# Context attention of a perceiver block: compacting a tile's outputs and repeating their sums by transfers through device memory

## The chip, the cores and the metric

The kernel runs on one core of one Trainium2 chip, as one program. The metric is the device time of one execution in microseconds (us); the median of several runs counts. A profile of one further execution comes with it; its times are from the start of its span.

## The reference, cut to what matters

Two layers of a perceiver work on 32 batches of 64 latent rows with 256 channels, with a context of 1601 rows of 256 channels for each batch. The second layer begins with the attention that this change is about:

```
q = layernorm(x) @ WqT + bq          # 64 rows per batch, 16 heads of 16
k = ctx @ WkT + bk                   # 1601 rows
v = ctx @ WvT                        # 1601 rows; bv is applied with the output projection
p = exp(q k / 4 - max)               # per head
o = (p v) / sum(p)                   # 64 rows x 16 heads x 16
x = x + (o + bv) @ WoT + bo
```

Before it stand a context mean, a self attention with 16 heads and a small routed feed-forward; behind it a recurrent mixer, a gated feed-forward and a quantised feed-forward. All of them run on the same engines, interleaved with the attention.

## The kernel before

**Tiles and steps.** Two batches make a tile of 128 rows, so there are 16 tiles. A tile's context is worked off in 13 steps (`NU = 13`): 12 steps of 512 context rows for one batch and one half of the heads, and one step (number 9) for the 65 rows that are left of both batches. The loop runs over 208 steps `g`; in the text a step is told by its number 0 to 12 within its tile.

**Inside a step**, in this order on every engine:

- `column_scores(g)`: the maxima as a first matmul (L773, tile `s`), then the scores with context rows on the partitions (L779), then two `Exp` by ScalarE into `pt` (L785).
- `values(g+4)`: eight fp32 matmuls into `vps` (L233), copied by VectorE into `vau` (L715). A head has 16 columns in `vau`, followed by a column of ones, so that the next product yields the head's sum as a 17th row.
- a piece of normalising in some steps (below), then pieces of the other layers that a plan puts here (`run(g, 0)`).
- `row_scores(g+5)`: scores with queries on the partitions (L731, tile `r`), reduced by VectorE to maxima `mx` (L738).
- `weighted(g)`: 32 small matmuls of `pt` with `vau` into `w.o` (L803), accumulated in PSUM over all steps of the tile.
- `keys(g+6)`: matmuls into `kps` (L233), copied with their bias into `kt` by ScalarE (L698).
- in step 1 the projection of the tile before, and further pieces of the plan (`run(g, 1)`).

**Order.** PE, VectorE, ScalarE and GpSimd keep the order in which the program writes their instructions; the order of the transfers on SP's queue is left to the scheduler. Each engine works in its order.

**PSUM.** `s` and `r` share two buffers of two banks (`ps_sc`), `w.o` has one bank (`ps_o`). Everything else (`vps`, `kps`, `sums`, `wo`, `hg`, `tpp` and so on) takes the next of three buffers in rotation (`ps_mm`), and a matmul into it waits until what lay in it three tiles ago has been read.

**Outputs of a tile.** `w.o` has four groups q, one for each batch and half of the heads; a group holds two sets m of four heads beside each other. Each head has 32 partitions, of which 16 are outputs, the 17th is the sum and 15 are not used. VectorE copies groups 0 to 2 to `osb` after step 9 (L808) and group 3 after step 12 (L810). `normalise(pos, q)` runs in steps 10, 11 and 12 for groups 0 to 2 and in step 0 of the next tile for group 3: a matmul with a 0/1 matrix `sel` repeats each sum over the 32 partitions of its head (L818, tile `sums`), VectorE takes reciprocals of 128x128 (L821) and multiplies (L822) into `oT`. `projected` then multiplies `oT` with `w_o2` in four matmuls (L838), because half of the 512 rows of `oT` and `w_o2` are padding, and adds the residue (L841). `out_bias` does the same once with the bias of the values (L830). At the end of the program, after step 12 of the last tile, group 3 is normalised and projected right away, and the last two tiles' second layers run off with nothing beside them.

**Loads.** SP issues the context (`ctxT`, 1.6 MB each), a second copy of it by halves (`part`, 800 KB) that ScalarE sums for the first layer's mean (L245), the 65 rows (`rest`), `x`, weights, and the output rows.

Of the kernel before, what the change touches and what calls it, by code (L numbers as in the profile page):

```python
# [9 lines left out]
F32 = mybir.dt.float32  # L10
BF16 = mybir.dt.bfloat16
AF = mybir.ActivationFunctionType
ALU = mybir.AluOpType
AX = mybir.AxisListType

P = 128
NB = 32
S = 64
D = 256
L = 1601  # L20
H = 16
NT = NB * S // P
# [6 lines left out]
NP = L // PIECE  # L29
TAIL = L - NP * PIECE  # L30
NU = 4 * NP + 1
# [7 lines left out]
BQ, BK, BV, BQ2, BK2, BV2, GC, GG, GF, DWB, DW = range(11)  # L39
# [5 lines left out]
def perceiver_kernel(ctx: ExitStack, tc: tile.TileContext, a: dict, out: bass.AP):  # L45
    nc = tc.nc
    PSUM = bass.MemoryType.PSUM

    const = ctx.enter_context(tc.tile_pool(name="const", bufs=1))
# [5 lines left out]
    loop = ctx.enter_context(ExitStack())  # L55
    big = loop.enter_context(tc.tile_pool(name="big", bufs=1))
    ps_sc = loop.enter_context(tc.tile_pool(name="ps_sc", bufs=2, space=PSUM))
    ps_o = loop.enter_context(tc.tile_pool(name="ps_o", bufs=1, space=PSUM))


# [8 lines left out]
    def mm_tile(shape, name, dtype=F32):  # L69
        return ps_mm.tile(shape, dtype, tag="mm", name=name)  # L70
# [32 lines left out]
    def load_rest(ti):  # L103

        t = big.tile([P, 2, 2, TAIL], F32, tag="rest", name=f"rest_{ti}", bufs=2)
        for b in range(2):
# [32 lines left out]

    onesb = const.tile([P, P], BF16, name="onesb")  # L140
    nc.vector.memset(onesb, 1.0)
    sel = const.tile([P, 4, 32], F32, name="sel")
    nc.gpsimd.affine_select(out=sel, in_=ones.rearrange("p (j r) -> p j r", j=4), compare_op=ALU.is_equal, fill=0.0,
                            base=-16, pattern=[[-32, 4], [0, 32]], channel_multiplier=1)


    dist = work_tile([P, S], "xn", "dist")
    for hb in range(2):
# [639 lines left out]
    def weighted(g):  # L788

        pos, h, k = split(g)  # L790
        w = wholes[pos]
        first, last = g % NU == 0, g % NU == NU - 1
        if first:
            w.o = o_tile([P, 4, 2, S], f"o1_{w.ti}")
        v, pts = vau[g % 5], w.pt.pop(g)
        kr = TAIL if h is None else P
        for j in range(4):
            q = j if h is None else h % 4
            for m in range(2):
                for c in range(4):  # L800
                    hd = 4 * m + c

                    nc.tensor.matmul(w.o[32 * c:32 * c + 32, q, m, :], lhsT=v[:kr, j, 17 * hd:17 * hd + 32],  # L803
                                     rhs=pts[m][:kr, c // 2, j, c % 2 * S:c % 2 * S + S],
                                     start=(m == 0 and (first and j == 0 or h is None and j == 3)), stop=(m == 1 and (last and j == 3 or h is None and j == 2)))
        if h is None:
            w.osb = work.tile([P, 4, 2, S], F32, tag="osb", name=f"osb_{w.ti}", bufs=1)
            nc.vector.tensor_copy(w.osb[:, 0:3], w.o[:, 0:3])  # L808
        elif last:
            nc.vector.tensor_copy(w.osb[:, 3], w.o[:, 3])  # L810

    def normalise(pos, q):

        w = wholes[pos]
        if q == 0:
            w.oT = work.tile([P, 2, 2, 2, S], F32, tag="oT1", name=f"oT1_{w.ti}", bufs=1)
        t = mm_tile([P, 2, S], f"sums_{w.ti}_{q}")
        nc.tensor.matmul(t.rearrange("p m s -> p (m s)"), lhsT=sel.rearrange("p j r -> p (j r)"),  # L818
                         rhs=w.osb[:, q].rearrange("p m s -> p (m s)"), start=True, stop=True)
        rs = work.tile([P, 2, S], F32, tag="rm", name=f"rs_{w.ti}_{q}", bufs=1)  # L820
        nc.vector.reciprocal(rs, t)  # L821
        nc.vector.tensor_tensor(w.oT[:, q % 2, :, q // 2, :], w.osb[:, q], rs, ALU.mult)  # L822

    def out_bias():

        bvb = work.tile([P, 4, P], F32, tag="oT1", name="bvb", bufs=1)
        nc.vector.tensor_copy(bvb, bv2.unsqueeze(2).to_broadcast([P, 4, P]))
        o = mm_tile([P, D], "bo2")
        for g in range(4):
            nc.tensor.matmul(o, lhsT=bvb[:, g, :], rhs=w_o2[:, g, :], start=(g == 0), stop=(g == 3))  # L830
        nc.vector.tensor_tensor(rows[:, R_BO2:R_BO2 + D], o, rows[:, R_BO2:R_BO2 + D], ALU.add)

    def projected(pos):

        w = wholes[pos]
        o = mm_tile([P, D], f"wo1_{w.ti}")
        for g in range(4):
            nc.tensor.matmul(o, lhsT=w.oT[:, g // 2, g % 2].rearrange("p b s -> p (b s)"), rhs=w_o2[:, g, :],  # L838
                             start=(g == 0), stop=(g == 3))
        x = work.tile([P, D], F32, tag="x4", name=f"x4_{w.ti}", bufs=1)  # L840
        nc.vector.tensor_tensor(x, o, residues[pos], ALU.add)  # L841
        return x
# [187 lines left out]
    w_s2 = load_w("L0_ffn_sw2T", D)  # L1030
    w_q2 = load_w("L1_xattn_WqT", D)


    w_o2 = const.tile([P, 4, D], F32, name="w_o2")
    bv2 = const.tile([P, 4], F32, name="bv2")
    nc.gpsimd.memset(w_o2, 0.0)
    nc.gpsimd.memset(bv2, 0.0)
    w_pw = const.tile([P, 2, D], F32, name="w_pw")
    w_hg = const.tile([P, 2, 2 * DI], F32, name="w_hg")
    w_go = const.tile([P, 4, 64], F32, name="w_go")  # L1040
# [6 lines left out]
    nc.gpsimd.memset(w_fo[:, NF - 1, :], 0.0)  # L1047

    def late_weights():
        for j in range(4):  # L1050
            nc.sync.dma_start(w_o2[32 * j:32 * j + 16],
                              a["L1_xattn_WoT"].rearrange("(g j d) o -> j d g o", j=4, d=16)[j])
            nc.sync.dma_start(bv2[32 * j:32 * j + 16], a["bv2"][j])
        nc.sync.dma_start(w_pw, a["L1_attn_pw_wT"].rearrange("(c p) o -> p c o", p=P))
        nc.sync.dma_start(w_hg, a["L1_attn_w_hg"].rearrange("(c h) d e -> (h d) c e", c=2))
        nc.sync.dma_start(w_go[:DI], a["L1_attn_w_out"].rearrange("h e o -> e h o"))
        for w, name in ((w_fg, "L1_attn_w_gate"), (w_fv, "L1_attn_w_value")):
            nc.sync.dma_start(w[:, :, :FF], a[name].rearrange("(c p) f -> p c f", p=P))
        last = (NF - 1) * P
        nc.sync.dma_start(w_fo[:, 0:NF - 1, :], a["L1_attn_w_ff_out"][0:last, :].rearrange("(f p) o -> p f o", p=P))  # L1060
        nc.sync.dma_start(w_fo[0:FF - last, NF - 1, :], a["L1_attn_w_ff_out"][last:FF, :])
# [160 lines left out]
    with tc.manual_schedule(engines={ET.PE, ET.DVE, ET.Activation, ET.Pool}):  # L1222
# [43 lines left out]
        for g in range(NU * NT):  # L1266
            pos, p = divmod(g, NU)
            if pos + 1 < NT:
                if p == 0:
                    wholes[pos + 1].rest = load_rest(order[pos + 1])  # L1270
                if p in (2, 9):
                    load_batch(2 * pos + 2 + p // 8)
            column_scores(g)
            if g + 4 < NU * NT:
                values(g + 4)
            if p == 0 and pos:
                normalise(pos - 1, 3)
            elif p > 3 * NP:
                normalise(pos, p - 3 * NP - 1)
            if g + 4 < NU * NT and scanned(g + 4)[2] == NP - 1:  # L1280
                maxima_rows(scanned(g + 4)[1])
            run(g, 0)
            if g + 5 < NU * NT:
                row_scores(g + 5)
                if scanned(g + 5)[2] == NP - 1:
                    maxima(scanned(g + 5)[1])
            weighted(g)
            if g + 6 < NU * NT:
                keys(g + 6)
            if p == 1 and pos:  # L1290
                x4[pos - 1] = projected(pos - 1)
            run(g, 1)
        normalise(NT - 1, 3)
        x4[NT - 1] = projected(NT - 1)
        plan.append(Steps(second_layer(NT - 1)))
        while plan:
# [6 lines left out]
def _layout(inputs):  # L1303

    import numpy as np

    g = {k: np.asarray(v) for k, v in inputs.items()}

    def t(v):
        return np.ascontiguousarray(v.T)  # L1310

    a = {
        "x": np.ascontiguousarray(g["x"].reshape(NB * S, D)),
        "ctxT": np.ascontiguousarray(g["ctx_1024"].transpose(0, 2, 1)),
        "L0_xattn_WT": t(g["L0_xattn_W"]),
    }
    for name in ("L0_attn_Wq", "L0_attn_Wk", "L0_attn_Wv", "L0_attn_Wo", "L0_ffn_w_gate", "L0_ffn_sw1",
                 "L0_ffn_sw2", "L0_ffn_sw3", "L1_xattn_Wq", "L1_xattn_Wk", "L1_xattn_Wv", "L1_xattn_Wo",
                 "L1_attn_pw_w", "L1_ffn_w1", "L1_ffn_w2"):
        a[name + "T"] = t(g[name])  # L1320
    for name in ("L1_attn_w_hg", "L1_attn_w_out", "L1_attn_w_gate", "L1_attn_w_value", "L1_attn_w_ff_out"):
        a[name] = np.ascontiguousarray(g[name])
    for name in ("w1", "w2", "w3"):
        a[name] = np.ascontiguousarray(g["L0_ffn_" + name])
    for k in range(4):
        g[f"dw{k}"] = g["L1_attn_dw_w"][:, 0, k]
    a["chv"] = np.ascontiguousarray(np.stack([g[n].reshape(2, P) for n in CH]).transpose(2, 1, 0))
    a["bv2"] = np.ascontiguousarray(g["L1_xattn_bv"].reshape(4, 4, 16).transpose(1, 2, 0))
    a["rows"] = np.concatenate([g[n] for n in ("L0_xattn_b", "L0_attn_bo", "L1_xattn_bo", "L1_attn_pw_b",
                                               "L0_ffn_expert_bias", "L0_attn_slopes")])  # L1330
    return a
# [16 lines left out]
```

## Time and profile before

| | |
|---|---|
| median of 3 runs | 2189.57 us (2186.16 to 2190.6) |
| the profiled execution's own time | 2185.15 us |
| its span | 2183.4 us, mean granted TensorE clock 0.977 |
| instructions | 69814 |
| `sums` matmuls (L818) | 64, two passes each |
| reciprocals (L821) and multiplies (L822) | 64 and 64 |
| projection matmuls (L838) | 64, two passes each |

The span runs from the first to the last instruction; the execution's own time has 1.75 us around it. PE is TensorE, PEld its weight loads (which overlap with PE), DVE is VectorE, ACT ScalarE, POOL GpSimd and SP the engine that issues the transfers. Groups of instructions are shown as line, engine, operation, output and input, count, then busy us, mean ns of one, and the idle time ahead of them with what ended it. The chain that ended last is followed back from the last instruction; its pieces are shown as start, us and what.

### The profile page before, as it was taken

How to read it: one execution, taken by the hardware profiler on the slowest of the kernel's cores; microseconds unless marked ns; L12 is line 12 of the kernel's file. 1: busy time of each engine (PE TensorE's matmuls, PEld its weight loads, DVE VectorE, ACT ScalarE, POOL GpSimd, SP SyncE). 2: the span in 40 equal slices, each digit the busy share in tenths (PEclk: the TensorE clock that was granted, in tenths of full speed). 3: DMA queues.
4: the chain of work that ended last, by engine and by line, in shares of the span. 5: the costliest groups of instructions: out<-in, count | busy, mean ns of one | idle time of the engine just before them, and what ended most of it. 6: DMA issues, size and time to landing. Idle time of an engine off the chain costs nothing.

```text
span 2183.4 us, 69814 instructions
## 1 busy us (share of the span) xinstructions
PE 2065.7 (95%) x31887; PEld 1510.1 (69%) x31903; DVE 1342.4 (61%) x2710; ACT 907.6 (42%) x1400; POOL 325.6 (15%) x541
## 2 busy tenths in 40 slices
PE   5799999999999999999999999999999999999984
PEld 3567677767677777777777676777777676677763
DVE  4556756666656766666666656566676665556554
ACT  3334444443535344454544435453433434334342
POOL 2111111111111111111111111111110111000011
PEclk8799999999999999999999999999999999999996
DMA  7233221211112121111211111110101101010000
GB/s 265 80 111 113 79 74 55 78 53 35 67 62 70 62 67 35 64 67 62 69 65 35 56 61 65 65 52 32 35 24 44 53 32 35 8 38 35 2 5 5
DMA packets 46176, 126.42 MB, mean 58 GB/s; under 512 B 12558, under 2 KB 28344, under 8 KB 45880
## 3 DMA queue, kind: packets, MB, share of 16 engines
q1 hardware_dynamic: 45320, 121.13, 16.2%
q8 instruction: 250, 4.10, 0.8%
q10 hardware_dynamic: 560, 0.81, 0.1%
q14 instruction: 46, 0.38, 0.1%
HBM read 119.83 MB, written 2.10 MB: 56 GB/s over the span
## 4 chain that ended last, share of the span: by engine, by line
PE 83%; DVE 11%; ACT 3%; issue 1%; DMA 1%; POOL 1%; SPq 0%; POOLq 0%; ACTq 0%; DVEq 0%
PE vps L233 16%; PE kps L233 15%; PE r L731 10%; PE o L803 9%; PE s L779 8%; PE ff L233 4%; DVE mx L738 3%; PE s L773 3%; PE ffo L946 2%; DVE vau L715 2%; PE q L233 1%; PE wo L838 1%; ACT pt L785 1%; PE hg L897 1%; PE v L319 1%
## 5 line engine op out<-in xcount | busy, mean ns | idle before, releaser
L738 DVE TENSOR_REDUCE mx<-r 128x2 f32<-128x1024 f32 x384 | 452.2, 1220 | 118.5 <-PE r L731 118.1
L785 ACT ACTIVATE pt<-s 128x1024 f32<-128x1024 f32 (+1 forms) x416 | 403.0, 1020 | 293.5 <-PE s L779 293.3
L698 ACT ACTIVATE kt<-kps,chv 128x512 f32<-128x512 f32 x192 | 131.9, 687 | 640.2 <-PE kps L233 640.2
L233 PE MATMUL vps<-w_L_xattn_WvT,ctxT 128*128 128x128 f32 x3072 | 395.1, 282 | 0.0
L233 PE MATMUL kps<-ctxT,w_L_xattn_WkT 128*128 128x512 f32 x768 | 383.2, 622 | 11.9 <-DMA ctxT<-ctxT 11.9
L233 PEld LDWEIGHTS vps<-w_L_xattn_WvT,ctxT 128*128 128x128 f32 x3072 | 359.0, 192 | 23.7 <-issue 2.8
L715 DVE COPY vau<-vps 128x512 f32<-128x512 f32 (+1 forms) x208 | 143.3, 689 | 373.0 <-PE vps L233 372.9
L803 PEld LDWEIGHTS o<-pt,vau 128*32 128x32 f32 (+1 forms) x13312 | 197.4, 110 | 150.9 <-issue 144.1
L803 PE MATMUL o<-pt,vau 128*32 128x64 f32 (+1 forms) x13312 | 232.0, 222 | 4.2 <-ACT pt L785 4.2
L731 PE MATMUL r<-kt,qbd 32*128 32x512 f32 x1536 | 228.1, 652 | 2.5 <-DVE mx L738 1.5
L233 PEld LDWEIGHTS kps<-ctxT,w_L_xattn_WkT 128*128 128x128 f32 x768 | 131.6, 191 | 123.7 <-issue 106.8
L779 PEld LDWEIGHTS s<-qbd,kt 32*128 32x128 f32 x6144 | 206.3, 187 | 3.1
L779 PE MATMUL s<-qbd,kt 32*128 32x128 f32 x6144 | 206.6, 271 | 0.0
L245 ACT ACTIVATE part<-part 128x1601 f32<-128x1601 f32 x60 | 92.6, 1543 | 15.8 <-DMA part<-ctxT 15.6
L731 PEld LDWEIGHTS r<-kt,qbd 32*128 32x128 f32 x1536 | 63.3, 185 | 40.9 <-issue 18.7
L773 PEld LDWEIGHTS <-onesb 3*128 3x128 bf16 x768 | 20.8, 91 | 91.3 <-issue 89.7
L773 PE MATMUL s<-neg,onesb 3*128 3x512 bf16 x768 | 79.0, 385 | 5.1 <-DVE mx L738 2.9
L821 DVE RECIPROCAL rs<-sums 128x128 f32<-128x128 f32 x64 | 60.7, 948 | 1.7 <-PE sums L818 1.7
L311 POOL TENSOR_TENSOR kbd<-kT,mask 128x512 f32<-128x512 f32 x32 | 32.9, 1049 | 138.0 <-ACT kT L304 138.0
L233 PE MATMUL ff<-nT,w_fg 128*128 128x128 f32 x384 | 51.6, 287 | 1.0 <-ACT nT L933 1.0
L233 PE MATMUL ff<-nT,w_fv 128*128 128x128 f32 x384 | 49.1, 278 | 0.0
L233 PEld LDWEIGHTS ff<-nT,w_fg 128*128 128x128 f32 x384 | 47.7, 200 | 1.8 <-ACT nT L933 1.6
(334 smaller groups left out, 2543.5 us busy)
## 6 DMA issues: line engine op xcount, KB each, us to landing
ctxT<-ctxT SPq DMA_DIRECT2D x32, 1601.0 KB, 7.1
part<-ctxT SPq DMA_DIRECT2D x60, 800.5 KB, 4.4
rest<-ctxT SPq DMA_DIRECT2D x32, 65.0 KB, 2.0
x<-x SPq DMA_DIRECT2D x16, 128.0 KB, 2.1
out<-x SPq DMA_DIRECT2D x16, 128.0 KB, 1.7
w<-w SPq DMA_DIRECT2D x16, 128.0 KB, 2.2
sum_L_ffn_w1T<-L_ffn_w1T SPq DMA_DIRECT2D x4, 256.0 KB, 6.6
raw_L_ffn_w1T<-L_ffn_w1T SPq DMA_DIRECT2D x4, 256.0 KB, 2.6
```

The costliest lines, as they stand in the source:

```text
L233: nc.tensor.matmul(o, lhsT=lhsT(c), rhs=rhs(c), start=(c == 0), stop=(c == 1))
L245: nc.scalar.activation(junk, src, AF.Copy, accum_out=csum[:, c, b:b + 1])
L698: nc.scalar.activation(kt, o, AF.Identity, bias=chv[:, hf.oc, BK2:BK2 + 1])
L715: nc.vector.tensor_copy(v[:kr, :, 0:VW - 16].rearrange("p k (h d) -> p k h d", d=17)[:, :, :, 0:16], o[:kr].rearrange("p k (h d) -> p k h ...
L731: nc.tensor.matmul(o, lhsT=qbd[r, q % 2, q // 2].rearrange("p h q -> p (h q)"), rhs=w.kt[r, q, :] if h is None else halves[h].kt[k][r, :], ...
L738: nc.vector.tensor_reduce(w.mx[:, 2 * m:2 * m + 2, h % 4, k], ps[m], AX.X, ALU.max)
L773: nc.tensor.matmul(o, lhsT=onesb[r, :], rhs=halves[h].neg[r, :].unsqueeze(1).to_broadcast([3, 4, P]), start=True, stop=False)
L779: nc.tensor.matmul(ps[i // 2][:kr, i % 2, j * P:(j + 1) * P], lhsT=w.kt[r, j, :] if h is None else halves[h].kt[k][r, j * P:(j + 1) * P], ...
L785: nc.scalar.activation(pt[:kr].rearrange("p i k c -> p i (k c)"), ps[m][:kr], AF.Exp)
L803: nc.tensor.matmul(w.o[32 * c:32 * c + 32, q, m, :], lhsT=v[:kr, j, 17 * hd:17 * hd + 32], rhs=pts[m][:kr, c // 2, j, c % 2 * S:c % 2 * S ...
L821: nc.vector.reciprocal(rs, t)
L946: nc.tensor.matmul(o, lhsT=m[:, f, :], rhs=w_fo[:, f, :], start=(f == 0), stop=(f == NF - 1))
```

## The change

The sums are no longer repeated by a matmul, and the outputs no longer stay in their padded layout. After the last copy to `osb`, in step 12, `gathered` issues five transfers on SP: one writes `osb` (128 x 512 numbers) to a buffer `od` in device memory; two read the 17th rows back, each repeated over 16 partitions, into `rs`; two read the 16 rows of outputs of each head back into `og`, without the padding. Each read fills 64 partitions with rows of 1 KB. `normalise` runs once for each tile, in step 1 of the next tile after the copy to `vau`: one reciprocal of 128x256 in place (L827 of the new kernel) and one multiplication of 128x256 (L829). `projected` needs two matmuls in place of four, since the 256 channels fill two chunks, and so does `out_bias`. `w_o2` is loaded in one transfer in place of four and needs no filling with zeros; `bv2` and `sel` go. At the end of the program `normalise` stands right behind `gathered` and the remaining pieces of step 12.

```diff
+    away = loop.enter_context(tc.tile_pool(name="away", bufs=2, space=bass.MemoryType.DRAM))
...
-            w.osb = work.tile([P, 4, 2, S], F32, tag="osb", name=f"osb_{w.ti}", bufs=1)
-            nc.vector.tensor_copy(w.osb[:, 0:3], w.o[:, 0:3])
+            w.osb = work.tile([P, 2, 4, S], F32, tag="osb", name=f"osb_{w.ti}", bufs=1)
+            nc.vector.tensor_copy(w.osb[:, :, 0:3], w.o[:, 0:3].rearrange("p q m s -> p m q s"))
         elif last:
-            nc.vector.tensor_copy(w.osb[:, 3], w.o[:, 3])
-
-    def normalise(pos, q):
+            nc.vector.tensor_copy(w.osb[:, :, 3], w.o[:, 3])
+
+    def gathered(pos):
         w = wholes[pos]
-        if q == 0:
-            w.oT = work.tile([P, 2, 2, 2, S], F32, tag="oT1", name=f"oT1_{w.ti}", bufs=1)
-        t = mm_tile([P, 2, S], f"sums_{w.ti}_{q}")
-        nc.tensor.matmul(t.rearrange("p m s -> p (m s)"), lhsT=sel.rearrange("p j r -> p (j r)"),
-                         rhs=w.osb[:, q].rearrange("p m s -> p (m s)"), start=True, stop=True)
-        rs = work.tile([P, 2, S], F32, tag="rm", name=f"rs_{w.ti}_{q}", bufs=1)
-        nc.vector.reciprocal(rs, t)
-        nc.vector.tensor_tensor(w.oT[:, q % 2, :, q // 2, :], w.osb[:, q], rs, ALU.mult)
+        w.og = work.tile([P, 4, S], F32, tag="og", name=f"og_{w.ti}", bufs=1)
+        w.rs = work.tile([P, 4, S], F32, tag="rm", name=f"rs_{w.ti}", bufs=1)
+        od = away.tile([P, 2, 4 * S], F32, tag="od", name=f"od_{w.ti}", bufs=2)
+        nc.sync.dma_start(od, w.osb.rearrange("p m q s -> p m (q s)"))
+        od = od.rearrange("(c r) m x -> c r m x", r=32)
+        for m in range(2):
+            r = slice(64 * m, 64 * m + 64)
+            nc.sync.dma_start(w.rs[r].rearrange("p q s -> p (q s)"), od[:, 16:17, m].to_broadcast([4, 16, 4 * S]))
+        for m in range(2):
+            r = slice(64 * m, 64 * m + 64)
+            nc.sync.dma_start(w.og[r].rearrange("p q s -> p (q s)"), od[:, 0:16, m])
+
+    def normalise(pos):
+        w = wholes[pos]
+        nc.vector.reciprocal(w.rs, w.rs)
+        w.oT = work.tile([P, 2, 2, S], F32, tag="oT1", name=f"oT1_{w.ti}", bufs=1)
+        nc.vector.tensor_tensor(w.oT.rearrange("p c b s -> p b c s"), w.og.rearrange("p (b c) s -> p b c s", c=2),
+                                w.rs.rearrange("p (b c) s -> p b c s", c=2), ALU.mult)
...
-        for g in range(4):
-            nc.tensor.matmul(o, lhsT=w.oT[:, g // 2, g % 2].rearrange("p b s -> p (b s)"), rhs=w_o2[:, g, :],
-                             start=(g == 0), stop=(g == 3))
+        mm2(o, lambda c: w.oT[:, c].rearrange("p b s -> p (b s)"), lambda c: w_o2[:, c, :])
...
-            if p == 0 and pos:
-                normalise(pos - 1, 3)
-            elif p > 3 * NP:
-                normalise(pos, p - 3 * NP - 1)
+            if p == 1 and pos:
+                normalise(pos - 1)
...
             weighted(g)
+            if p == NU - 1:
+                gathered(pos)
...
-        normalise(NT - 1, 3)
+        normalise(NT - 1)
         x4[NT - 1] = projected(NT - 1)
```

More of the change, by code (lines that the diff above doesn't have):

```diff
@@ L141, in perceiver_kernel @@
     nc.vector.memset(onesb, 1.0)
-    sel = const.tile([P, 4, 32], F32, name="sel")
-    nc.gpsimd.affine_select(out=sel, in_=ones.rearrange("p (j r) -> p j r", j=4), compare_op=ALU.is_equal, fill=0.0,
-                            base=-16, pattern=[[-32, 4], [0, 32]], channel_multiplier=1)
     dist = work_tile([P, S], "xn", "dist")
@@ L824, in out_bias @@
     def out_bias():
-        bvb = work.tile([P, 4, P], F32, tag="oT1", name="bvb", bufs=1)
-        nc.vector.tensor_copy(bvb, bv2.unsqueeze(2).to_broadcast([P, 4, P]))
+        bvb = work.tile([P, 2, P], F32, tag="oT1", name="bvb", bufs=1)
+        nc.vector.tensor_copy(bvb, chv[:, :, BV2:BV2 + 1].to_broadcast([P, 2, P]))
         o = mm_tile([P, D], "bo2")
-        for g in range(4):
-            nc.tensor.matmul(o, lhsT=bvb[:, g, :], rhs=w_o2[:, g, :], start=(g == 0), stop=(g == 3))
+        mm2(o, lambda c: bvb[:, c, :], lambda c: w_o2[:, c, :])
@@ L836, in projected @@
         o = mm_tile([P, D], f"wo1_{w.ti}")
-        for g in range(4):
-            nc.tensor.matmul(o, lhsT=w.oT[:, g // 2, g % 2].rearrange("p b s -> p (b s)"), rhs=w_o2[:, g, :],
-                             start=(g == 0), stop=(g == 3))
+        mm2(o, lambda c: w.oT[:, c].rearrange("p b s -> p (b s)"), lambda c: w_o2[:, c, :])
         x = work.tile([P, D], F32, tag="x4", name=f"x4_{w.ti}", bufs=1)
@@ L1031, in perceiver_kernel @@
     w_q2 = load_w("L1_xattn_WqT", D)
[L1034 to L1037, printed above, removed]
+    w_o2 = const.tile([P, 2, D], F32, name="w_o2")
     w_pw = const.tile([P, 2, D], F32, name="w_pw")
@@ L1049, in late_weights @@
     def late_weights():
[L1050 to L1053, printed above, removed]
+        nc.sync.dma_start(w_o2, a["L1_xattn_WoT"].rearrange("(c p) o -> p c o", p=P))
         nc.sync.dma_start(w_pw, a["L1_attn_pw_wT"].rearrange("(c p) o -> p c o", p=P))
@@ L1327, in _layout @@
     a["chv"] = np.ascontiguousarray(np.stack([g[n].reshape(2, P) for n in CH]).transpose(2, 1, 0))
-    a["bv2"] = np.ascontiguousarray(g["L1_xattn_bv"].reshape(4, 4, 16).transpose(1, 2, 0))
     a["rows"] = np.concatenate([g[n] for n in ("L0_xattn_b", "L0_attn_bo", "L1_xattn_bo", "L1_attn_pw_b",
```

## The prediction

> **What bounds the kernel now.** I read the page's busy times first, then the chain of work that ended last (its shares, and its pieces inside single steps), then the groups by line with shapes kept apart, then the DMA issues.
>
> ```profile
> PE 2065.7 (95%) x31887; PEld 1510.1 (69%) x31903; DVE 1342.4 (61%) x2710; ACT 907.6 (42%) x1400; POOL 325.6 (15%) x541
> PE 83%; DVE 11%; ACT 3%; issue 1%; DMA 1%; POOL 1%; SPq 0%; POOLq 0%; ACTq 0%; DVEq 0%
> ```
>
> TensorE is full and holds 83% of the chain; VectorE holds 11% with 61% busy. So an edit pays what it takes off PE's sequence, or off those places where PE waits for VectorE. The chain's pieces show three kinds of steps around the removed `sums` matmul (start us, us, what):
>
> ```profile
> 1100.11 0.22 PE sums L818 x2
> 1100.33 1.07 PE r L731 x8
> ...
> 1091.03 0.70 DVE vau L715
> 1091.73 0.04 issue
> 1091.78 1.11 PE hg L897 x14
> ...
> 329.28 0.69 DVE vau L715
> 329.97 0.87 DVE rs L821
> 330.87 0.29 DVE oT L822
> 331.16 2.28 DVE mx L738 x2
> ...
> 1128.12 1.73 PE wo L838 x8
> ```
>
> First: `sums` itself is on the chain, 0.22 us. Second: it was issued 0.31 us before 1091.03, but the chain waits for VectorE's copy `vau`: the three PSUM buffers of `ps_mm` turn over, and with `sums` taking one, the second `hg` tile gets the buffer of `vps`, which is free only when `vau` is done. Third: the chain runs through the normalising itself (reciprocal L821, multiply L822) into `mx`. The last line is the projection: 8 passes (two for each fp32 matmul) in 1.73 us, all on the chain.
>
> ```profile
> L821 DVE RECIPROCAL rs<-sums 128x128 f32<-128x128 f32 x64 | 60.7, 948 | 1.7 <-PE sums L818 1.7
> L363 DVE RECIPROCAL rs<-sm 128x16 f32<-128x16 f32 x15 | 3.8, 253 | 0.5
> L474 DVE TENSOR_TENSOR gt<-gt,lower 128x256 f32<-128x256 f32 x4 | 1.7, 425 | 0.1
> rest<-ctxT SPq DMA_DIRECT2D x32, 65.0 KB, 2.0
> out<-x SPq DMA_DIRECT2D x16, 128.0 KB, 1.7
> raw_L_ffn_w1T<-L_ffn_w1T SPq DMA_DIRECT2D x4, 256.0 KB, 2.6
> ```
>
> These price what is added: the two reciprocal rows give (948-253)/112 = 6.2 ns per element, and the DMA rows (us from issue to landing) the transfers.
>
> **Removed: 64 `sums` matmuls.** Four belong to the last tile's end, 60 to the loop. I went through the chain in each of the 60 steps. In 18 it passes through `sums`: 0.22 us each, less about 0.02 because `r` may then wait for ACT's `pt` (that wait exists in the trace: 14 times, 6.0 us): 18 x 0.2 = 3.6 us. In 14 it passes through L821 and L822. VectorE loses 1.24 us there (948+293 ns), but PE is close behind: before the next column scores PE stood idle 0.76 us where the shortest such gap is 0.33, so 0.43, plus the 0.2 of `sums` itself: 14 x 0.6 = 8.4. In 28 it passes through `vau` and back to PE, as in the second example. Without `sums` each following tile moves one buffer earlier in the rotation: the built program shows the second `hg` tile waiting for `kt` of the last keys, long done, in place of `vau`. At most 0.77 us (1091.01 to 1091.78) is freed, at least the 0.2 of the matmul; in some steps a second tile (`o` of L385, `tp_b`) then meets `vau` instead. I take 0.5: 28 x 0.5 = 14. Together 26 us; the bounds are 60 x 0.2 = 12 and 4 + 9 + 28 x 0.77 = 34.
>
> **Halved: the projection.** Four of 8 passes at 0.216 us are 0.865 us, in 15 tiles of the loop 13.0 us. But the normalising is now one piece in front of it, in step 1 of the next tile, right behind `vau`: a 128x256 reciprocal, 948 + 128 x 6.2 = 1742 ns, and a 128x256 multiply, 425 ns (the L474 row): 2.17 us that VectorE did not have in this step. Queued behind it: `mx`, which frees the score buffers for the next column scores. In the tile at 998 us `vau` ends at 998.84 and `mx` at 1001.79; `mx` moves to 1003.96, while the column scores, 0.865 earlier, want the second buffer at 1003.33: 0.63 us lost. The same sum over the 15 tiles (idle time ahead of `mx` taken off) gives 1.13, 0.63 four times, 0.19, 0.08, and nothing in the other 8: 3.9 us. So 13.0 - 3.9 = 9.1. In steps 10, 11, 12 and 0 VectorE is lighter by 1.24 us each; that is in the 26.
>
> The Trainium skill, "TensorE: Matmul & The Clock Gate", section "Back-to-back issue gap", gives 262 cycles at 2.4 GHz, 109 ns, for 256 columns alone. By that figure half the projection would be 0.44 us and 6.5 us in all in place of 13.0; the row of 8 passes in 1.73 us decides, and the rest stands without this.
>
> **Added: five transfers per tile on SP's queue.** `od` (256 KB out) waits for the last `osb` copy; two reads of `rs` and two of `og` (64 KB each) wait for `od`. Nothing in the trace writes and reads back. I take 2.6 for `od` (the 256 KB row; 1.7 is the lower bound, from the only row that writes to device memory), 2.0 for a read (the 65 KB row), 0.43 for each further issue on SP, 0.1 for each hand-over: `rs` complete 0.1 + 2.6 + 0.1 + 0.43 + 2.0 = 5.2 us after `osb`, `og` 0.9 later, which the reciprocal of 1.74 hides. The cover: from the end of `osb` to the end of `vau` in step 1 the trace has 12.05 us in the tightest tiles (1112.13 to 1124.18), 16.5 in the widest, 14.3 in the mean. In four tiles an 800 KB `part` was issued 1.2 us before `osb` was ready (1366.06 against 1367.26); it lands in 4.4, so `od` may take 3 us more, 8.4 in all: still covered. If the cover were gone, VectorE would stand in front of `mx`, and PE behind it.
>
> SP's order in the built program: every transfer ahead of `od` was issued before `osb` was done, every one behind it after, in all tiles. Behind it wait at the nearest `x` (472.16 us, 2.0 after `osb`; read 109 us later) and a ternary piece (232.76, 7.1 after): neither is held to harm. I cost them at nothing.
>
> **The end.** Here nothing covers the trip.
>
> ```profile
> 2110.65 0.88 DVE rs L821
> 2111.55 0.30 DVE oT L822
> 2111.90 1.15 PE wo L838 x4
> ```
>
> `osb` is done at 2109.51, so the reciprocal starts at 2114.7 in place of 2110.57: 4.1, plus 0.8 for the longer reciprocal and 0.1 for the multiply. PE's last part of `wo` stays as it is. VectorE is in order, so both tails behind it move: +5.0 us. Bounds: 4.1 with a 1.7 us `od`, 9 if both landings take the 4.4 of the 800 KB row.
>
> **At the start.** `out_bias` loses two matmuls, 0.9 us. Eight small loads become one, and the fills of `w_o2`, `bv2` and `sel` go: SP and POOL are not on the chain there, nothing. The `osb` copies keep their sizes (549 and 282 ns).
>
> **Sum:** -26 - 9.1 - 0.9 + 5.0 = -31.0 us. The profiled execution took 2185.15 us (span 2183.4), 4.4 under the median 2189.57. So 2154.2 against the profiled execution and 2158.6 against the median, which I forecast.
>
> **Rivals.** *The gaps close again:* the freed waits come back on the next tile in the rotation or on ACT's `pt`, and only issue time is saved: -12 - 9.1 - 0.9 + 5.0 = -17, 2172.6 us. For it: `r` already waits for `pt` in many steps. Against: the chain shows `vau` as the one late thing in the 28 steps.
>
> *Slower: the round trip outlasts its cover.* With a trip of T from `osb` to `rs`, each of 15 tiles loses T - 14.3 and the end T - 0.2; against a gain of 36.0 this breaks even at 16T = 36 + 214.7, T = 15.7. At 17 us: 15 x 2.7 + 16.8 - 36 = +21, 2211 us. For it: loads that collide land in 8.8 to 10.9 us at the start of the trace, and two such in series are 18 to 22. Against: the DMA engines are little used around a tile's end (1% in 329 to 346 us, 15% in 1099 to 1116, 19% in 1366 to 1381). The Trainium skill, "DMA: Bandwidth & Descriptors", section on the anatomy of one DMA, says that completion can take "a surprisingly long delay especially when the write target is HBM"; the `out` row with 1.7 us bears out no such delay here.
>
> *VectorE takes over step 1:* the lump of 2.17 us eats all of the halved projection: -26 - 0.9 + 5.0 = -21.9, 2167.7 us. For it: the 3.9 us above leave little room in 5 tiles; against: 8 tiles have 0.24 to 2.3 us of room after the lump.
>
> **Chances.** Forecast 0.57, gaps close 0.22, VectorE in step 1 0.12, slower 0.07, a mixture that cancels 0.02. The forecast's own bounds: best 34 + 13 + 0.9 - 4.1 = -44, 2146; worst, 12 us from `sums`, nothing from the projection, 9 at the end: -4, 2186. The range is 2146 to 2184: it leaves out the slower case and the last edge. About 0.2% (4 us) is what can be told from no change: faster 0.91, same 0.02, slower 0.07.
>
> **What would show it.** After: L827 (reciprocal) 16 times at 1.7 us, and no idle time of VectorE ended by a DMA there, apart from one wait of about 4 us at the end; `hg` no longer waiting for `vau`; the chain's `wo` halved, its `vau` share down from 39 us by half; `mx` in step 1 ending last before some column scores. Wrong would be: a wait for `rs` or `og` in every tile, `od` landing above 10 us, or PE's busy time falling without the span.

## The result, and the profile after

| | before | after |
|---|---|---|
| median of 4 runs each on one chip | 2187.86 us (2183.2 to 2190.6) | 2155.52 us (2154.58 to 2156.67) |
| the profiled execution's own time | 2185.15 us | 2154.58 us |
| its span, clock | 2183.4 us, 0.977 | 2152.9 us, 0.974 |

The ratio is 0.9853 with an interval of 0.9838 to 0.9868: faster by 32.3 us in the medians and by 30.6 us between the two profiled executions. The forecast was 31.0 less and 2158.6 us.

The page of after, busy times and shares of the chain:

```profile
PE 2034.8 (95%) x31691; PEld 1482.9 (69%) x31707; DVE 1302.2 (60%) x2614; ACT 907.1 (42%) x1400; POOL 324.7 (15%) x538
PE 84%; DVE 9%; ACT 3%; DMA 2%; issue 1%; POOL 1%; SPq 0%; POOLq 0%; DVEq 0%; ACTq 0%
```

PE is busy for 30.9 us less (2065.7 to 2034.8), and the span fell by 30.5; VectorE's share of the chain fell from 11 to 9%, DMA's rose from 1 to 2%. The chain of after in the tile of the prediction's first examples, steps 10, 11 and 1 of the next tile (start us, us, what):

```profile
1071.63 1.98 PE vps L230 x16
1073.61 1.05 PE hg L902 x16
...
1079.94 1.98 PE vps L230 x16
1081.92 1.20 PE r L728 x8
...
1109.55 0.86 PE wo L230 x4
```

Before, 0.77 us lay between the end of `vps` and `hg`, `vau` among it; now `hg` follows at once, and in the waits of the weight loads the line of `hg` for `vau` is gone (before 14 times, 5.5 us). In step 11 the 0.22 of `sums` is gone, but `r` takes 1.20 in place of 1.07: 0.09 is gained there, not 0.2. The projection is 0.86 in place of 1.73. By pieces of the whole chain `vau` fell from 38.9 to 12.5 us (57 pieces to 24), by two thirds rather than half.

The new VectorE instructions by source line (ns min/median/max, first and last start), then VectorE's and PE's waits in after (engine, line, waited for; us in total, times, longest):

```profile
L827 DVE RECIPROCAL rs<-rs x16: 1741/1743/1753, 237.6 to 2078.0; 128x256 f32<-128x256 f32 x16
L829 DVE TENSOR_TENSOR oT<-og,rs x16: 424/424/426, 239.4 to 2079.8; 128x256 f32<-128x256 f32 x16
```

```profile
DVE rs L827 <- DMA rs<-od: 4.2, 1, 4.2
```

```profile
PE s L770 <- DVE mx L735: 4.5, 9, 0.7
```

Sixteen reciprocals of 1.74 us, and one single wait of VectorE for the transfers, 4.2 us at the end: as the prediction said. The column scores (`s`, its first matmul) wait for `mx` 9 times in place of 5: the lump of step 1 is late there. And the end of the program, the chain from the last `osb` on:

```profile
2071.82 2.67 DMA od<-osb
2074.58 0.54 SPq L819
2075.17 2.72 DMA rs<-od
2077.98 1.76 DVE rs L827
2079.77 0.44 DVE oT L829
2080.25 2.09 PE wo L230 x4
2082.43 0.43 DVE x L846
```

From the end of `osb` (2071.80) to the residue add `x` are 10.6 us; before it was 3.6 (2109.51 to 2113.14). The change gives back 7.0 us here. The last `osb` itself came 37.7 us earlier than before.

**Where the time went, by steps.** Each step has one copy to `vau`. From its end in one step to its end in the next, summed over tiles 1 to 14, the traces give (us; the kernels e2 to e12 are those of the experiments):

| step | before | after | e2 | e12 | e9 | e8 | e3 | e4 | e5 | e10 | e11 |
|---|---|---|---|---|---|---|---|---|---|---|---|
| 10 | 146.3 | 135.6 | 139.5 | 146.0 | 146.0 | 135.9 | 135.6 | 135.6 | 135.6 | 135.6 | 135.6 |
| 11 | 118.4 | 114.3 | 116.6 | 116.6 | 115.6 | 117.7 | 114.3 | 114.3 | 114.3 | 114.3 | 114.3 |
| 12 | 142.2 | 130.8 | 133.3 | 138.3 | 138.2 | 133.4 | 130.8 | 130.8 | 130.8 | 130.8 | 130.8 |
| 0 | 124.0 | 119.9 | 122.2 | 123.1 | 123.2 | 121.1 | 119.9 | 121.5 | 149.2 | 119.9 | 119.9 |
| 1 | 144.0 | 137.4 | 137.3 | 137.3 | 138.9 | 137.3 | 144.7 | 130.7 | 132.0 | 140.5 | 207.2 |
| the other 8 | 1114.6 | 1115.2 | 1116.9 | 1114.0 | 1117.0 | 1115.9 | 1114.1 | 1116.1 | 1114.6 | 1113.3 | 1114.8 |

What the kernels share repeats to 0.1 us in steps 10 to 12 and 0; in the other eight steps sums differ by up to 4 us from run to run, nearly all of it in steps 7 and 8, which no edit touches. Much of that is the granted clock of TensorE: the traces' records of it have stretches of 3.4 us at 0.50, now in one step and now in another, and one such stretch makes its step some 1.6 us longer (step 7 of tile 8 in e2, e4 and e5, and in no other kernel). So differences below read from single steps are sharper than those of the medians. Steps 10, 11, 12 and 0 fell by 30.3 us, step 1 by 6.6, the rest not at all.

A copy to `vau` can itself come late because VectorE is busy, without PE losing anything. Where this matters, a step is counted below from the end of its last `vps` matmul on PE to that of the next step. The four steps then fall by 30.2 us and step 1 by 6.6, nearly the same.

### The profile page after: what moved, and what is told of

The parts are those of the page before. It is cut to its first block, busy times and chain, and to the rows that moved or that the text cites. A ratio compares the mean times of both kernels' runs of the same rounds, so it can differ in the third digit from the quotient of the medians.

```text
span 2152.9 us, 69473 instructions
## 1 busy us (share of the span) xinstructions
PE 2034.8 (95%) x31691; PEld 1482.9 (69%) x31707; DVE 1302.2 (60%) x2614; ACT 907.1 (42%) x1400; POOL 324.7 (15%) x538
## 4 chain that ended last, share of the span: by engine, by line
PE 84%; DVE 9%; ACT 3%; DMA 2%; issue 1%; POOL 1%; SPq 0%; POOLq 0%; DVEq 0%; ACTq 0%
PE vps L230 17%; PE kps L230 16%; PE r L728 10%; PE o L800 9%; PE s L776 8%; PE ff L230 4%; DVE mx L735 3%; PE s L770 3%; PE ffo L951 2%; PE q L230 1%; ACT pt L782 1%; PE wo L230 1%; PE hg L902 1%; PE s L330 1%; PE v L316 1%
## 5 line engine op out<-in xcount | busy, mean ns | idle before, releaser
L230 PEld LDWEIGHTS kps<-ctxT,w_L_xattn_WkT 128*128 128x128 f32 x768 | 132.0, 191 | 124.4 <-issue 107.5
L230 PEld LDWEIGHTS ff<-nT,w_fv 128*128 128x128 f32 x384 | 46.5, 196 | 0.0
```

Source lines behind the costliest of these rows:

```text
L230: nc.tensor.matmul(o, lhsT=lhsT(c), rhs=rhs(c), start=(c == 0), stop=(c == 1))
```

## The experiments

All of them are edits of the kernel after, whose 2155.5 us they are held against; the ratio is that to before. They ran on three chips, on which before took 2187.9, 2189.6 and 2189.2 us, so differences of medians are sure to about 2 us, and the readings rest on the steps. Theory: the 26 us predicted for `sums` are mostly a held PSUM buffer, the reciprocals count little, step 1 loses a few us to the lump of VectorE, and the transfers are hidden but for the end. Rivals: it is the matmul's own time; it is VectorE's lighter load; the transfers cost something in every tile.

**e1_buffer: only take the PSUM tile.** In steps 10, 11, 12 and 0 a tile of `ps_mm` is asked for, which nothing writes or reads.

```diff
+    def again(pos, q):
+        mm_tile([P, 2, S], f"sums_{wholes[pos].ti}_{q}")
...
+            if p == 0 and pos:
+                again(pos - 1, 3)
+            elif p > 3 * NP:
+                again(pos, p - 3 * NP - 1)
```

> The changed kernel, but in steps 10, 11, 12 and 0 it takes one PSUM buffer of the rotation of three and does nothing with it: no matmul, no work for VectorE. It shares everything else with the changed kernel (2155.5 us). Theory (about 14 of the 26 us come from the rotation: tiles after vps no longer wait for vau): 8 to 16 us slower than the changed kernel, 2164 to 2171; hg waits for vau again in 14 or 15 steps, and vau holds over 30 us of the chain instead of 12.5. Rival (only the issue time of the sums matmuls was saved): within 2 us of the changed kernel.

Measured: 2155.54 us (2154.47 to 2157.37), 0.9859 [0.9846, 0.9872], and step by step the times of after, to 0.1 us. The expectation failed, and it says nothing on the wait: the instructions and waits that came out are those of after. The prediction's "three buffers turn over in rotation" was wrong. A tile that nothing uses holds no buffer; that a tile gets the buffer that came free first fits this run and the next, and was not tested further. As a run it is a repetition of after.

**e2_sums: the matmul back, its result unread.** The same places, with `sel` and

```diff
+        t = mm_tile([P, 2, S], f"sums_{w.ti}_{q}")
+        nc.tensor.matmul(t, lhsT=sel.rearrange("p j r -> p (j r)"), rhs=w.osb[:, :, q], start=True, stop=True)
```

> The changed kernel with the sums matmul back in steps 10, 11, 12 and 0: it takes its PSUM buffer and PE's time, and nobody reads it. Theory (in most steps the matmul is hidden while the next tile waits for vau): 3 to 7 us above the run with the idle buffer alone. Rival (the buffer does not matter and the matmul is paid in full): 60 x 0.22 = 13 us above the changed kernel and above the run with the idle buffer.

Measured: 2168.42 us (2166.07 to 2171.85), ratio 0.9919 [0.9906, 0.9932]: 12.9 more than after. In the four steps it is 11.0 us for 56 matmuls, 0.20 each; nobody reads the tile, so it is free at once, and `hg` doesn't wait for `vau`, which it would in a strict rotation. The matmul's own time is paid in full, and it is a third of the 30.3.

**e8_vector: VectorE's work back, without matmul.** A reciprocal of a 128x128 constant and a multiplication, unread, in the same steps.

```diff
+        t = work.tile([P, 2, S], F32, tag="spare", name=f"spare_{w.ti}_{q}", bufs=1)
+        nc.vector.reciprocal(t, ones.rearrange("p (m s) -> p m s", m=2))
+        nc.vector.tensor_tensor(t, w.osb[:, :, q], t, ALU.mult)
```

> The changed kernel with VectorE's part back in steps 10, 11, 12 and 0: a 128x128 reciprocal of a constant and a 128x128 multiply with osb, unread, 1.24 us each time; no matmul and no PSUM buffer. Theory (in 14 of 60 steps the chain went through this work, and PE is close behind): 5 to 9 us slower than the changed kernel. Rival (VectorE has room everywhere): within 2 us. Rival (the reciprocals were the bound in all of these steps): over 30 us slower.

Measured: 2160.72 us (2159.4 to 2163.66), 0.9884 [0.987, 0.9898]: 5.2 more, in the four steps 7.5. Of these 2.9 lie in a single step, number 12 of tile 13, where the granted clock is 0.50 for 3.4 us, as in before and not in after.

**e9_held: hold the buffer, with next to no work.** A matmul of one column into a tile of `ps_mm`, and a VectorE copy of one number out of it, which stands behind `vau`.

```diff
+        t = mm_tile([P, 2, S], f"held_{w.ti}_{q}")
+        nc.tensor.matmul(t[0:1, 0, 0:1], lhsT=onesb[:, 0:1], rhs=onesb[:, 0:1], start=True, stop=True)
+        c = small.tile([1, 1], F32, tag="spare", name=f"spare_{w.ti}_{q}", bufs=1)
+        nc.vector.tensor_copy(c, t[0:1, 0, 0:1])
```

> The changed kernel; in steps 10, 11, 12 and 0 a matmul of one column takes a PSUM buffer and a copy of one number by VectorE, where the reciprocal stood, reads it. So the buffer is held as the sums tile held it, with next to no work. (An idle buffer made no difference at all, 2155.54 us: the pool gives out the buffer that came free first, so a buffer that nobody uses holds nothing.) Theory (the sums matmul alone cost 12.9 us, VectorE's part 5.2; about 11 us of what the loop gained are left for the held buffer): 6 to 13 us slower than 2155.5, and hg waits for vau again in most steps 10. Rival (the rest comes from the two acting together, the buffer alone does nothing): 0 to 3 us slower.

Measured: 2181.61 us (2179.5 to 2183.92), 0.9968 [0.9956, 0.998]: 26.1 more, far over the expectation. In the four steps it is 22.4; the rest lies in step 1 (1.5, in one tile with 3.4 us at a granted clock of 0.50) and in what varies. The two new instructions (ns min/median/max, first and last start), and the waits of the weight loads, where `hg` waits again for VectorE in 14 steps:

```profile
L828 PE MATMUL held<-onesb x63: 164/164/165, 200.0 to 2094.3; 128*1 128x1 bf16 x63
L830 DVE COPY spare<-held x63: 134/134/147, 200.7 to 2094.5; 1x1 f32<-1x1 f32 x63
```

```profile
PEld hg L910 <- DVE spare L830: 7.3, 14, 0.5
```

A matmul of 0.16 us and a copy of 0.13 us bring back three quarters of what the removal gained, because the third buffer is taken until VectorE has come past `vau`. What the short matmul costs without its hold was not run; in step 10, though, this kernel and the next, with the full matmul, lose the same to 0.01 us in every tile, so there the length of the matmul does not count.

**e12_sums_held: both.** e2's matmul, with e9's copy of one number.

> The changed kernel with the full sums matmul back in steps 10, 11, 12 and 0, and a copy of one number by VectorE that holds its PSUM buffer as the reciprocal did. The matmul without the hold cost 12.9 us, the hold with a matmul of one column 26.1 us. Theory (the two overlap: while the next tile waits for vau the matmul runs for nothing, and only where nothing waits is it paid): 1 to 4 us above the held buffer alone, 2182 to 2186. Rival (the costs add): 7 us or more above it, 2189 or more.

Measured: 2177.4 us (2176.69 to 2178.11), 0.9943 [0.9928, 0.9958]: 21.9 more, in the four steps 23.4. So the costs do not add (11.0 and 22.4), as the theory held against the rival, and it lies even below the theory's bounds. In step 10 of the tile shown above the chain of this kernel reads:

```profile
1085.34 0.69 DVE vau L715
1086.03 0.06 DVE spare L833
1086.09 1.10 PE hg L913 x14
...
1094.41 0.22 PE sums L831 x2
```

Before `hg` the matmul is off the chain, hidden while PE waits for `vau`; in the next step it is on it. In step 10 this kernel has the time of before to 0.01 us in 14 of 15 tiles: after gains 0.60 to 0.86 us there in every tile, and this is the matmul with its hold alone, none of it VectorE's work but for 0.22 in one tile.

**e3_project4: the projection twice.** The pair of matmuls is issued once more, so the projection has its old eight passes behind the new lump.

```diff
         mm2(o, lambda c: w.oT[:, c].rearrange("p b s -> p (b s)"), lambda c: w_o2[:, c, :])
+        mm2(o, lambda c: w.oT[:, c].rearrange("p b s -> p (b s)"), lambda c: w_o2[:, c, :])
```

> The changed kernel with the two projection matmuls of a tile issued twice, so four as before; the second pair starts the sum anew. Theory (half the projection gives 13.0 us of PE time in the loop, of which VectorE's lump of reciprocal and multiply takes 3.9 back): about 9 us slower than the changed kernel, 2164 to 2166. Rival (the lump costs nothing): 13 us slower or more. Rival (the lump eats all of it): 0 to 3 us slower.

Measured: 2163.77 us (2163.61 to 2165.14), 0.9897 [0.9884, 0.991]: 8.2 more. Step 1 rises by 7.3 us in 14 tiles: by 0.81 to 0.87, all or nearly all of the four passes, in six, by 0.20 in four where PE waits for `mx` behind the lump, by nothing in two, and by 0.64 and 0.74 in the other two. So the lump does eat part of the halved projection: four passes in 14 tiles are 12.1 us, and 4.8 of them are hidden behind it.

**e4_end_of_0: the normalising one step earlier,** behind `weighted` at the end of step 0, when that step's `mx` is already done.

```diff
-            if p == 1 and pos:
-                normalise(pos - 1)
...
             weighted(g)
+            if p == 0 and pos:
+                normalise(pos - 1)
```

> The changed kernel with the normalising moved from step 1 (behind vau) to the end of step 0 (behind weighted), some 4 us earlier. Theory (the lump of 2.17 us delays mx in step 1 and takes 3.9 us of the halved projection back; VectorE is idle at the end of step 0, and rs and og have landed by then): 3 to 6 us faster than 2155.5. Rival (the transfers land too late there, at 8 us after osb): slower, with a wait of VectorE for rs in many tiles. Rival (the lump cost nothing): within 1 us.

Measured: 2149.59 us (2146.05 to 2150.91), 0.9817 [0.9804, 0.983]: 5.9 less. In the table step 1 falls by 6.7 and step 0 rises by 1.6, but the 1.6 is only the border: in tiles 5 and 12 VectorE comes to `vau` 0.7 us late, and PE doesn't wait for it. The copy of step 1 of tile 5 in after, right behind its `vps` (end 729.85), and in e4, 0.8 us behind (end 729.61):

```profile
729.88 0.69 DVE L712 COPY vau<-vps 128x512 f32<-128x512 f32 x1 [0.87 <-PE vps L230]
```

```profile
730.38 0.68 DVE L712 COPY vau<-vps 128x512 f32<-128x512 f32 x1
```

Counted on PE, step 0 stays as it is and step 1 falls by 5.1 us in 14 tiles. VectorE waits for the transfers of the loop practically nowhere (`og` once, 0.3 us), though the reciprocal starts 7.9 to 11.4 us after `osb` in place of 12.5 to 16.2.

**e5_early_0: earlier still,** in step 0 right behind `vau`.

```diff
-            if p == 1 and pos:
+            if p == 0 and pos:
                 normalise(pos - 1)
```

> The changed kernel with the normalising in step 0 right behind vau, 5.1 to 7.1 us after osb. Theory (a trip of about 5.2 us, 7.4 in the four tiles with an 800 KB load ahead): waits of 0 to 0.5 us in 10 to 12 tiles and about 2 us in three or four, in all 0 to 8 us slower than 2155.5. Rival (a trip is longer than that beside the loads, 8 us or more): a wait of 3 us or more in every tile, over 25 us slower.

Measured: 2181.39 us (2176.32 to 2189.58), 0.9969 [0.9951, 0.9988]: 26 more, well over the expectation. That is the size of the rival, but not its condition: in the loop VectorE waits 19.3 us for `rs`, more than 3 us in one tile only. The clock adds to it: between 200 and 2060 us it is 0.50 for 24 us, in after for 3.4. Step 0 rises by 29.3. VectorE's waits and the chain in tile 1's end:

```profile
DVE rs L827 <- DMA rs<-od: 24.2, 13, 6.0
```

```profile
343.46 2.03 DMA od<-osb
...
345.51 0.53 SPq L819
...
346.10 2.84 DMA rs<-od
...
349.03 1.76 DVE rs L827
```

With the cover gone the whole trip is seen: `od` lands in 2.0 us, not 2.6, and is no slow write; but SP takes 0.53 for the issue of a read, and the reads land in 2.8, not 2.0. The reciprocal starts 5.5 to 6.8 us after `osb` in quiet tiles, against 5.2 in the prediction, and 7.7 to 8.3 (once 11.2) where an 800 KB `part` is ahead, against 8.4. The Trainium skill, "DMA: Bandwidth & Descriptors", section on the anatomy of one DMA, fits a transfer (one that GpSimd issues) as 2.0 us and its bytes by 436 thousand a us, which is 2.6 for this write of 256 KB and 2.15 for a read of 64 KB; the trace has 2.03 and 2.84, so the write to device memory, of whose delay the page warns, is under its fit here, and the read above it.

**e10_two_trips and e11_three_trips: a longer trip.** `osb` is written, read back whole, and written again before the five transfers follow; e11 does this twice.

```diff
-        nc.sync.dma_start(od, w.osb.rearrange("p m q s -> p m (q s)"))
+        src = w.osb.rearrange("p m q s -> p m (q s)")
+        for k in range(1):                                     # e11: range(2)
+            far = away.tile([P, 2, 4 * S], F32, tag=f"far{k}", name=f"far{k}_{w.ti}", bufs=2)
+            nc.sync.dma_start(far, src)
+            src = work.tile([P, 2, 4 * S], F32, tag="near", name=f"near{k}_{w.ti}", bufs=1)
+            nc.sync.dma_start(src, far)
+        nc.sync.dma_start(od, src)
```

> The changed kernel with the way through device memory gone twice: osb is written, read back whole, written again, and then read as rs and og. A trip is then about 10 us, 12 with an 800 KB load ahead. Theory (a cover of 12.5 to 16 us in the loop, none at the end): nothing in the loop, 5 us more at the end, 2160 to 2162. Rival (the cover is nearly used up, or SP's queue is held up behind the transfers): over 2170.

Measured: 2163.08 us (2161.05 to 2167.96), 0.9884 [0.9869, 0.99]: 7.6 more. The reads of `rs` are issued 6.6 to 12.1 us after `osb`, in place of 2.0 to 4.5, and still VectorE waits for `rs` only twice (8.3 us at the end and 1.1 in the loop); step 1 rises by 3.1 over 14 tiles. At least 4.5 us more of trip are covered in nearly every tile.

> The changed kernel with the way through device memory gone three times. A trip is then about 15 us (the two-trip run had its last reads issued 6.6 to 12 us after osb, the reads take 3.5 to 4.7), 17 or more with an 800 KB load ahead; the cover is 12.5 to 16. Theory of the prediction's slower rival (break-even with the kernel before at a trip of 15.7): nearly all of the gain is gone, 2175 to 2192. Other theory (waits of VectorE in step 1 are soaked up by slack of PE): 2168 or less.

Measured: 2242.11 us (2231.14 to 2245.61), 1.0223 [1.0189, 1.0257]: slower than before, and 86.6 more than after, which neither theory had. The direction is that of the prediction's slower rival, the size is not. The mean start of the reciprocal in the loop is 17.3 us after `osb`, 3.2 later than the mean end of `vau` in front of it (14.1): by the rival's formula 15 x 3.2 = 48, and 8.8 at the end, 57 together. Step 1 rose by 69.8 in 14 tiles. One of them in the chain, and PE's work there by the timeline (start us, us, the instructions, idle time before and what ended it):

```profile
1152.67 4.16 DMA og<-od
...
1156.96 0.43 DVE oT L835
...
1157.93 2.25 DVE mx L735 x2
```

```profile
1157.53 1.23 PE L230 MATMUL wo<-w_o,oT 128*128 128x256 f32 x4 [2.54 <-DVE oT L835]
1159.10 0.61 PE L770 MATMUL s<-neg,onesb 3*128 3x512 bf16 x2 [0.34 <-DVE mx L735]
...
1162.48 3.34 PE L230 MATMUL vps<-w_L_xattn_WvT,ctxT 128*128 128x128 f32 x16
```

Two things come on top of the wait for `rs`. `og` lands after `rs` (11 waits of VectorE for it, 7.9 us in all). And after PE stood idle for 2.54 us the granted clock is 0.50: the windows of this kernel give 1.00 for 1150 to 1156, 0.80 to 1160, 0.50 to 1164 and 0.90 to 1170, and the 16 passes of `vps` take 3.3 us in place of 2.0. Such a stall is paid twice. Over the loop the clock is 0.50 for 72 us here and for 3.4 in after; by our estimate, half of the difference, that is up to 34 us of lost work, enough for the 30 that the formula lacks. How much is the clock and how much `og` was not separated.

**e7_both: what the steps point to.** e4's place for the normalising, and the last tile done on the chip as before (its sums by `sel`, padded weights `w_o4`, four matmuls, no transfer).

```diff
+            if pos == NT - 1 and p > 3 * NP:
+                normalise_last(p - 3 * NP - 1)
...
-            if p == NU - 1:
+            if p == NU - 1 and pos < NT - 1:
                 gathered(pos)
+            if p == 0 and pos:
+                normalise(pos - 1)
...
-        normalise(NT - 1)
+        normalise_last(3)
```

> The kernel with the normalising at the end of step 0 (2149.6 us), and the last tile alone done on the chip as in the kernel before: four sums matmuls, four reciprocals and multiplies, four projection matmuls with padded weights, no transfer. Theory (the last trip is uncovered: osb to x took 3.6 us before and 10.6 after): 7 us faster, 2141 to 2144. Rival (the time at the end goes to the slower TensorE clock behind it in both): less than 3 us faster.

Measured: 2145.23 us (2144.77 to 2146.32), 0.9797 [0.9782, 0.9811]: 10.3 less than after and 4.4 less than e4, a little short of the expected 7. It beats both kernels. Its end:

```profile
2069.82 0.53 PE sums_last L833 x2
2070.35 2.97 PE wo L860 x8
...
2073.42 0.44 DVE x L865
```

The residue add starts 4.5 us after `osb` (2068.9) in place of 11.0 in e4; against that the last `osb` is 1.7 us later, with the last tile's `sums` matmuls back and the varying step 8 2.5 us longer.

## Why the prediction was right, point by point

| term of the sum | predicted | measured |
|---|---|---|
| 60 `sums` matmuls in the loop | -26 | -32.0 |
| halved projection | -13.0 | -12.5 (before less e4, step 1 of 15 tiles) |
| given back to the lump in step 1 | +3.9 | +5.2 (after less e4, the same steps) |
| `out_bias` | -0.9 | -1.0 (step 3 of the first tile) |
| end | +5.0 | +7.0 |
| sum | -31.0 | -33.3 |
| not in the sum: the start, and steps without an edit | 0 | +2.7 |
| profiled executions | | -30.6 |

The loop's terms are counted on PE, from `vps` to `vps`. That the total came within half a microsecond is partly luck: 6 us more from `sums` than predicted were set off by 1.8 less in step 1, 2.0 more at the end and 2.7 that the sum does not have.

**`sums`.** Right in its mechanisms and 6 us short in one of them. The prediction's three kinds of steps are found in the trace of before as it counted them. The 28 through `vau` gained 21.8 us, 0.78 each, for the 14 predicted; e12 takes 19.8 of these back, so they are the matmul and its hold. The 18 through the matmul gained 3.0 for 3.6. The 14 through VectorE gained 7.2 for 8.4, but 2.9 of this is step 12 of tile 13, where before has a granted clock of 0.50 for 3.4 us and after has not; the other 13 gained 0.33 each for the 0.6 predicted, so this term came out by luck.

The step that was mis-sized is "I take 0.5" for a step that runs through `vau`: step 10 gained 0.60 to 0.86 in all 15 tiles, around the upper bound of 0.77 that the prediction had worked out from one gap. Its reservation, that a second tile would meet `vau` instead, did not come true there. The words "rotation" and "one buffer earlier" were wrong (e1, e2); the wait follows from who holds a buffer and for how long. In step 11 its 0.2 was too much in some tiles (0.05 to 0.23 by e2), since `r` takes some of it back.

By causes, in the 56 steps of 14 tiles, the gain of 30.3 divides into the matmul alone 11.0 (e2), the hold on top of it 12.4 (e12), and VectorE's work 6.9 (the rest; alone 7.5 in e8). The prediction implies 60 x 0.2 for the matmul, 28 x 0.3 for the hold and 14 x 0.4 for VectorE; for 56 steps this is 11.2, 7.8 and 5.2. The shares of matmul and hold depend on the order in which they are put back: the hold with the short matmul of e9 is 22.4, and the full matmul adds 1.0 to it.

**The projection and the lump.** The four passes came out as worked out (0.86 in 13 of 15 tiles). The lump costs 5.2, not 3.9, and the difference is for the most part one tile. By tiles (after less e4, step 1) it is 0.66 four times where the prediction has 0.63 four times, 0.22 for 0.19, 0.13 and 0.12 for 0.08, and 1.18 and 1.17 where it has a single 1.13; in one tile after gains 0.28. e3 agrees, with 4.8 us of the four passes hidden in 14 tiles. The rival "VectorE takes over step 1" had the mechanism and two fifths of its size: 5.2 of 12.5.

**The transfers.** Hidden in all 15 tiles, with the one wait at the end, as forecast; there is room for a reciprocal 4.6 us earlier (e4) or for reads issued 4.5 us later (e10). The parts of the trip were wrong in both directions: `od` 2.0 for 2.6, a read's issue on SP 0.5 for 0.43, its landing 2.7 to 2.8 for 2.0. At the end, `od` took 2.67.

**The end.** +7.0 for +5.0: the reads and their issue make about 1 us of the difference (the reciprocal starts 6.2 us after `osb`, 5.1 later than before, for 4.1), PE the other. The prediction said that "PE's last part of `wo` stays as it is"; its four passes take 2.09 us in place of 1.15 before and 0.86 in the loop, at a granted clock of 0.50. The clock had fallen at 2071.4 us, in the first row below, 1.9 us before PE's long idle stretch began, and in e7, without a trip, it fell at 2069.3; in before it fell at 2115.7, behind `wo`. So it is not shown that the trip brought it down (windows of after: start and end, length, busy times and counts of PE, PEld, DVE, ACT and POOL, PE's clock, DMA share, GB/s):

```profile
2070.00:2072.00 2.00, 1.55 (x59) 1.46 (x60) 0.29 (x1) 0.40 (x1) 0.00 (x0) 0.86 0.04 8
2072.00:2080.00 8.00, 1.31 (x7) 1.12 (x6) 2.41 (x3) 0.51 (x2) 1.51 (x3) 0.50 0.19 66
2080.00:2083.00 3.00, 2.08 (x4) 1.18 (x4) 0.73 (x3) 0.00 (x0) 0.00 (x0) 0.50 0.00 0
```

**The start.** `out_bias` lies in step 3 of the first tile, which is 0.96 us shorter in every kernel with the change, as predicted. But step 1 of that tile is 1.35 longer: the granted clock is 0.50 for 6.8 us in it, in before for 3.4 (from 116 to 119 us it is 0.50 in after and 1.00 in before). e7, which also has 3.4 us there, takes the time of before to 0.02 us. The first copy of step 0 starts 0.7 later (99.39 for 98.70 us; among the kernels it varies by 3 us). With the 0.6 by which the other eight steps of the table differ, these make 2.6 of the 2.7 us that the sum does not have. What sets the clock there stays open.

**The rivals.** "The gaps close again" is out: e2 gives its size, 11 to 13 us for the matmul alone, and after gained 30. "The round trip outlasts its cover" is a true threshold, seen in e11, but its price there is half again that of the formula.

## What to carry to other kernels

Price a PSUM buffer by how long it is held: a matmul whose result waits for a busy engine costs its successor that wait, and its own time is then free (step 10 of e9 and e12), so the two are not to be added. A round trip through device memory is cheap where 12 us of other work lie between write and use, and is the first thing to take out where nothing lies there. Leaving out the padding and joining four small VectorE pieces into one saves work (2.17 us for 4.96 in a tile), but the place of the joined piece must be chosen anew: behind the instruction that others wait for, not in front of it.

## What the hardware showed that was not expected

- The granted clock fell to 0.50 with no long idle stretch of PE ahead of it. In after, at the end, it fell at 2071.4 us, when PE had had gaps of 1.2 us at most in the 10 us before; the idle stretch of 6.94 us (2073.31 to 2080.25) came behind. It rose again at 2088.5, after 8.3 us of renewed work, and four passes took 2.09 us in place of 0.86. In before, in the middle of the loop, it fell at 1893.8 for 3.4 us after gaps of 0.37 and 1.00 us. In e11 it fell at 1158.4, 0.8 us after an idle stretch of 2.54 us had ended, and rose at 1165.2. The Trainium skill, "TensorE: Matmul & The Clock Gate", section "Why this matters for your kernels", advises against idle gaps of over about 3 us for this reason; all three falls came after shorter ones.
- Of a trip through device memory the write was the quick part (2.0 us for 256 KB), the reads of 64 KB the slow one (2.7 to 2.8 us, two pairs behind each other, 0.5 us of SP for each issue).
